# A gated attention stage: gates summed by a VectorE scan in place of triangle products, rows turned by DMA, and VectorE's work in another order

## The chip, the core and the metric

The kernel runs on one core of a Trainium2 chip. A core has five engines that run side by side, each with its own queue of instructions: TensorE (PE; its weight loads are listed as PEld), VectorE (DVE), ScalarE (ACT), GpSimd (POOL) and SyncE (SP), which here issues transfers. The metric is the device time of one execution in microseconds.

## The reference, cut to what matters

The model is two layers over x (16 batches of 256 tokens by 256 features). Layer 0 is a cross attention and an expert layer, layer 1 another cross attention and a gated linear attention. Only the last is touched by the change:

```python
gk1 = log_sigmoid(x @ Wg1a @ Wg1b + bg1) / 16      # first stream's gates, per token, head, feature
gk2 = log_sigmoid(x @ Wg2a @ Wg2b + bg2) / 16      # second stream's gates
fac, mfac = ...                                     # one of four experts per token, by softmax(x @ We)
o_dense  = gla(q1, k1, v, gk1)
o_sparse = sum over experts of gla(q2 * fac, k2 * fac, v, gk2 * mfac)
o = o_dense + o_sparse
o = o * rsqrt(mean(o * o) + eps) * norm_w * (g * sigmoid(g)),  g = x @ Wga @ Wgb
x = x + tanh(g_ffn[1]) * (o @ Wo)
```

`gla` is a linear attention with decays: with G the sum of the gates along the tokens up to t, the weight of token s for token t is (q exp(G_t)) . (k exp(-G_s)), for s at or before t. A constant added to all of G cancels, so the sum may start anywhere.

## The kernel before, in words

The stages run one after another, with the ends laid over each other; the last one is `stage3_fast` (from L1619). It treats one batch after another, and in each batch four pairs of heads; one pair is a step, `p` counts them from 0 to 63, `b = p // 4` is the batch and `m = p % 4` the step within it. All instructions of this stage are kept in the order in which the program issues them, on each engine, so the order written out in the loop `for p in range(last)` and in the tables `start`, `copies`, `middle`, `rest`, `late`, `behind_mask`, `by_rows` and `logs` (L2007 on) is the order of every engine's queue. A table entry such as `(route, 1)` under key 1 means: in step 1 of a batch, do `route` for the batch one ahead. Products are float32; the profile counts two instructions for each.

What a batch needs ahead of its steps is made during the steps of the batch before, or of the one before that:

- `stats` and `norm_ahead` give the normed rows `xn`, two batches ahead: VectorE's moments, four small POOL operations, then ScalarE's scaling. `turn_ahead` turns them to `xnT` (features by tokens) by sixteen VectorE transposes of 32 rows each.
- `lows` (step 0) multiplies `xnT` by the small first factors, and VectorE copies the result to `low`. A quarter of it is also wanted on other partitions: two VectorE operations make `low2`, and a transfer makes `lowd`.
- `all_gates` (step 1), `gates_end` and `gate_logs` (steps 1 and 2) make `lg` = log(1 + exp(-z)) for both streams, with tokens on the partitions. `steepest` keeps its largest entry for a check at the end of the kernel.
- `route_rows`, `route_logits` and `route_sums` (step 0) and `route` (step 1) choose the expert of each token, `turn_hot` and `turned_hot` (step 2) turn that choice, and `pairs` (step 2) makes the masks `em` (pairs of tokens of one expert, with the triangle) and `am`.
- `outgates` makes the output gate: four products, then ScalarE's exponents and copies `zs`, later a POOL product `gw`.

Within step p, TensorE goes through `keys_queries(p + 1)`, `decays(p + 1)`, the first stream's scores `products(p, 0)`, `values(p - 1)` (in steps 1 to 3, by `inside`), `second(p + 1)`, the second stream's scores `products(p, 1)`, and in step 0 only then `values` of the pair before. `decays` sums the gates by products: the gates `lg` are the weights and a triangle of -1/16 and 1/16 (`dmask`, 128 by 128 for each half of the tokens) is multiplied in for the first stream, `em` for the second; four ScalarE exponents read the two results from PSUM. VectorE multiplies the keys and queries by them (`factors`, `f`; `factors_second`, `q`), and POOL the second stream's keys (`k`). `masked(p, 0)` takes the first scores out of PSUM (VectorE, `at`), which frees the only bank pair `sc` for the second scores; `masked(p, 1)` takes those (four VectorE operations) in step p + 1, and POOL adds the two (`at<-at,at`) before `values(p)` can read them. `squares`, `gated`, `scaled` and `project` finish a batch in the steps of the next one.

Of the kernel before, what the change touches and what calls it, by code (L numbers as in the profile page):

```python
# [10 lines left out]
F32 = mybir.dt.float32  # L11
# [6 lines left out]
P = 128  # L18
# [36 lines left out]
def flamingo_kernel(tc: tile.TileContext, t, out):  # L55


    nc = tc.nc
    with tc.tile_pool(name="flag", bufs=1) as fp:
        check = {n: fp.tile(shape, F32, tag=n, name=n) for n, shape in (  # L60
            ("esum", [P, 2 * S]), ("rsum", [P, S]), ("most", [P, 2 * B]), ("uneven", [P, B]),
            ("gates", [P, 2 * B]), ("second", [P, 16]), ("logs", [P, 2 * B]),
            ("rows", [P, 2, 8]), ("rsum2", [P, 2 * B]), ("rsum0", [P, 4 * B]))}
        for x in check.values():
            nc.gpsimd.memset(x, 0.0)
        bad = check["bad"] = fp.tile([1, 1], I32, tag="bad", name="bad")
        layers(tc, t, out, check)
        with tc.If(nc.values_load(bad[0:1, 0:1], min_val=0, max_val=P,
                                  skip_runtime_bounds_check_because="a count of partitions") > 0):
            layers(tc, t, out, None)  # L70
# [3 lines left out]
def layers(ctx: ExitStack, tc: tile.TileContext, t, out, check):  # L74
# [1544 lines left out]
    def stage3_fast(early_bank):  # L1619

        with ExitStack() as sx:
# [25 lines left out]
            nc.sync.dma_start(out=lbg2[64:], in_=t["lbg"][:64, :])  # L1647
            low2 = w1.tile([64, P], F32, tag="low2", name="low2")
            wo = w1.tile([P, 4, D], F32, tag="wo", name="wo")

            hots = [w1.tile([P, 2, 4], F32, tag=f"hot{n}", name=f"hot{n}") for n in range(2)]

            xn, xnT, low, lg, hT, em, am, lowd = {}, {}, {}, {}, {}, {}, {}, {}
            v, gw, u_, oT = {}, {}, {}, {}
# [17 lines left out]
            def norm_ahead(b):  # L1672
                xn[b] = w0.tile([P, 2, D], F32, tag="xn", name="xn")
                normed(xn[b], xs[b], *mvs.pop(b))

# [8 lines left out]
            def turn_ahead(b):  # L1684

                xnT[b] = of(b).tile([P, 2, S], F32, tag="xnT", name="xnT")
                turned_squares(xnT[b], xn[b], range(16))

            def lows(b):

                low[b] = of(b).tile([P, 2, S], F32, tag="low", name="low")
                ps = bank("low")
                for c in range(2):
                    for k in range(2):
                        matmul(ps[:, c * S:(c + 1) * S], la[:, k, c * P:(c + 1) * P], xnT[b][:, k, :],
                                         start=k == 0, stop=k == 1)
                dve3.tensor_copy(low[b][:, 0, :], ps[:, :S])
                dve3.tensor_scalar(low[b][:, 1, :], ps[:, S:], vec[:, V_ONE:V_ONE + 1], None, ALU.add)
                lowd[b] = of(b).tile([P, S], F32, tag="lowd", name="lowd")
                nc.sync.dma_start(out=lowd[b][64:], in_=low[b][:64, 1, :])  # L1700
                if b > 0:
                    for r in range(0, 64, 32):
                        dve3.tensor_scalar(low2[r:r + 32, :], ps[64 + r:96 + r, S + P:],
                                           vec[64 + r:96 + r, V_ONE:V_ONE + 1], None, ALU.add)

# [38 lines left out]

            def gates(b, i):

                if i == 0:
                    lg[b] = of(b).tile([P, 2, 2, 512], F32, tag="lg", name="lg")
                for n, (lo, hi) in enumerate(((64, 81), (96, 113))):
                    ps = bank("z")  # L1750
                    matmul(ps, low[b][lo:hi, 1, tokens(i)], lbg[lo:hi, :], start=True, stop=True)
                    act3.activation(lg[b][:, i, n, :], ps, AF.Exp, scale=-1.0)

            def all_gates(b):

                lg[b] = of(b).tile([P, 2, 2, 512], F32, tag="lg", name="lg")
                two = psa.tile([P, 2, 512], F32, tag="sc", name="sc")
                one = [bank("z"), bank("z")]
                for i in range(2):
                    for n, (lo, hi) in enumerate(((0, 17), (32, 49))):  # L1760
                        x, w = (low2[lo:hi, :], lbg2[lo:hi, :]) if i else (low[b][64 + lo:64 + hi, 1, tokens(0)],
                                                                         lbg[64 + lo:64 + hi, :])
                        matmul(two[:, n, :] if i else one[n], x, w, start=True, stop=True)
                act3.activation(lg[b][:, 0, 0, :], one[0], AF.Exp, scale=-1.0)
                act3.activation(lg[b][:, 1], two, AF.Exp, scale=-1.0)
                z_[b, "z"] = one[1]

            def gates_end(b):
                act3.activation(lg[b][:, 0, 1, :], z_.pop((b, "z")), AF.Exp, scale=-1.0)

            def gate_logs(b, i):
                act3.activation(lg[b][:, i], lg[b][:, i], AF.Ln, bias=1.0)

            def steepest(b, i):
                dve3.tensor_reduce(check["gates"][:, 2 * b + i:2 * b + i + 1],
                                        lg[b][:, i].rearrange("p n f -> p (n f)"), AX.X, ALU.max)

# [29 lines left out]
            def outgates(b):  # L1807
# [7 lines left out]
                for h, ps in enumerate(two):  # L1815
                    e, zs = (w2.tile([P, 512], F32, tag=n, name=n) for n in ("eg", "zs"))
                    act3.activation(e, ps, AF.Exp, scale=-1.0)
                    act3.copy(zs, ps)
                    z_[b, h] = zs, e
# [22 lines left out]
            def decays(p):  # L1842

                b, m, cols = place(p)
                gq[p] = psu.tile([P, 512], F32, tag="gq", name="gq")
                gz[p] = psu.tile([P, 512], F32, tag="gz", name="gz")
                for n, (ps, mask) in enumerate(((gq[p], dmask), (gz[p], em[b]))):
                    for i in range(2):
                        matmul(ps[:, tokens(i)], lg[b][:, i, n, cols], mask[:, i, :], start=True, stop=True)
                    ee[p, n] = w2.tile([P, 2, S], F32, tag=f"ee{n}", name=f"ee{n}")  # L1850
                    act3.activation(ee[p, n][:, 0, :], ps[:, :S], AF.Exp)
                    act3.activation(ee[p, n][:, 1, :], ps[:, :S], AF.Exp, scale=-1.0)

# [23 lines left out]
            def shares_end(b):  # L1877
# [4 lines left out]
                flat = rd[b].rearrange("p x j -> p (x j)")  # L1882
                most = check["second"].rearrange("p (x j) -> p x j", j=2)
                dve3.tensor_tensor(most, most, den[:, :, 0::16], ALU.max)
                dve3.reciprocal(rd[b], den[:, :, 0::16])
# [64 lines left out]
            def squares(b, mp):  # L1950
                if mp == 0:
                    u_[b] = w2.tile([P, 4, S], F32, tag="u", name="u")
                    oT[b] = w2.tile([P, 4, S], F32, tag="oT", name="oT")
                ps = o.pop((b, mp))
# [50 lines left out]

            start = {2: [(turn_hot, 1)]}
            copies = {2: [(turned_hot, 1)]}  # L2007
            middle = {0: [(lows, 1)], 1: [(all_gates, 1)], 2: [(pairs, 1)], 3: [(scaled, 0, 0)]}

            rest = {0: [(bias, 2)], 1: [(route, 1)], 2: [(steepest, 1, 0), (stats, 2)], 3: [(steepest, 1, 1), (turn_ahead, 2)]}  # L2010
            late = {1: [(scaled, -1, 1)], 2: [(project, -1)], 3: [(vals, 1)]}
            behind_mask = {0: [(route_logits, 1)]}
            by_rows = {0: [(outgates, 0)], 1: [(gates_end, 1)]}
            logs = {0: [(route_sums, 1), (outgates_end, 0, 0)], 1: [(outgates_end, 0, 1), (gate_logs, 1, 0)], 2: [(gate_logs, 1, 1), (norm_ahead, 2)]}

# [15 lines left out]
            keys_queries(0)  # L2031
            for f, *a in ((turn_hot, 0), (turned_hot, 0), (stats, 1), (pairs, 0), (norm, 1), (steepest, 0, 0),
                          (steepest, 0, 1)):
                f(*a)
# [21 lines left out]
            for p in range(last):  # L2056
# [5 lines left out]
                if 0 < p:  # L2062
                    masked(p - 1, 1)
                run(copies, p)
                if p % 4 == 0:
                    shares_end(p // 4)
                if 1 < p and p % 2 == 1:
                    gated((p - 2) // 4, (p - 2) % 4 // 2)
# [13 lines left out]

                inside = p % 4 > 0 and p + 1 < last
                if inside:
# [17 lines left out]
            gated(b, 1)  # L2102
            ends.part("rsum", "gates", "rsum2", "rsum0")
            scaled(b, 1, dve3, [lambda: project_part(b, 1, 0), warm])
# [5 lines left out]
    class Verdict:  # L2110

        bounds = {"esum": E_MOST, "rsum": R_MOST, "most": E_MOST, "uneven": 0.5, "second": E_MOST, "logs": E_MOST,
                  "gates": G_MOST, "rows": ROWS + 0.5, "rsum2": R_MOST, "rsum0": R_MOST}

        def __init__(self):
            self.r, self.n = st.tile([P, 10], F32, tag="vr", name="vr"), 0

# [103 lines left out]
```

## Time and profile before

| | us |
|---|---|
| median of 3 runs (1840.51 to 1845.21) | 1845.09 |
| the profiled execution's own time | 1847.08 |
| its span, first to last instruction | 1845.3 |
| TensorE, VectorE busy in the span | 1813.5, 1231.5 |
| ScalarE, GpSimd busy in the span | 873.9, 1017.0 |
| a batch of the last stage, 1457.97 to 1495.68 | 37.71 |

The profile is of one execution. In a row of the groups, `x64` is the number of instructions, then come the busy time of all, the mean nanoseconds of one, and the idle time just before them with what ended it. An arrow names what is written and what is read. Nearly all lines are helpers (L50, L1637, L1640), so the names of the tiles tell which step of the program a row is. The chain is the work that ended last, followed back. In the timeline a row is start, length, engine, line, operation, and in square brackets the idle time before it. TensorE's instructions overlap: a product that lasts 0.38 us in its row may follow the one before by 0.11, so a run of products is measured by what it advances the chain.

### The profile page before, as it was taken

The page shows a single profiled execution, that of the slowest core. Times are in us where ns is not written, and L with a number is a line of the kernel's source. Part 1 is how long each engine was busy: PE and PEld are TensorE (multiplying, and loading weights), DVE is VectorE, ACT ScalarE, POOL GpSimd, SP SyncE. Part 2 cuts the span into 40 slices and gives each one's busy share as a digit, 9 for nine tenths or more (in the row PEclk, how much of TensorE's full clock was granted, in tenths as well). Part 3 has the DMA queues.
Part 4 walks back from the last instruction along what each step waited for, and adds up shares of the span by engine and source line. Part 5 has one row for each costly group of instructions (what it writes and reads, how often), then busy time and mean ns, then how long its engine had stood idle before and what let it go on. Part 6 is the DMA issues. An engine that isn't in the chain of part 4 may idle for free.

```text
span 1845.3 us, 35182 instructions
## 1 busy us (share of the span) xinstructions
PE 1813.5 (98%) x13870; PEld 1249.8 (68%) x13870; DVE 1231.5 (67%) x2903; ACT 873.9 (47%) x1804; POOL 1017.0 (55%) x1001
## 2 busy tenths in 40 slices
PE   8999999999999999999999999999999999999997
PEld 5666666666766667666777766656767777777765
DVE  3355656566665666656474488867888878878874
ACT  4433344433444334443433487846555645455543
POOL 4654767567676576756634767315444444444433
PEclk9999999999999999999999999999999999999999
DMA  9800010000010100000077933100000000000000
GB/s 304 226 1 22 16 34 15 25 17 23 23 37 8 29 19 10 31 23 18 13 248 238 233 49 49 18 4 3 14 8 10 8 10 13 8 9 8 14 9 14
DMA packets 68504, 85.86 MB, mean 47 GB/s; under 512 B 10740, under 2 KB 55908, under 8 KB 67818
## 3 DMA queue, kind: packets, MB, share of 16 engines
q1 hardware_dynamic: 56041, 66.74, 11.5%
q0 software_dynamic: 12288, 16.79, 4.5%
q8 instruction: 111, 1.82, 0.4%
q14 instruction: 64, 0.52, 0.1%
HBM read 44.17 MB, written 38.29 MB: 45 GB/s over the span
## 4 chain that ended last, share of the span: by engine, by line
PE 82%; POOL 9%; DVE 4%; issue 2%; ACT 2%; DMA 1%; SPq 0%; POOLq 0%; DVEq 0%; ACTq 0%
PE o L50 11%; PE qk L50 11%; PE v L50 8%; PE sc L50 8%; PE proj L50 7%; PE kq L1637 7%; PE sc L1637 5%; POOL es L50 4%; PE gq L1637 3%; PE v L1637 3%; PE o L1637 3%; PE proj L1637 3%; POOL x L50 2%; PE ex L50 2%; POOL rs L50 2%
## 5 line engine op out<-in xcount | busy, mean ns | idle before, releaser
L50 POOL TENSOR_SCALAR rs<-mv 128x2 f32<-128x2 f32 (+2 forms) x85 | 16.3, 192 | 376.8 <-DVE mv L50 371.1
L50 DVE RECIPROCAL rd<-o 128x256 f32<-128x256 f32 x64 | 112.3, 1755 | 164.0 <-PE o L50 123.7
L50 POOL TENSOR_TENSOR at<-at,at 128x768 f32<-128x768 f32 x63 | 114.1, 1812 | 142.4 <-DVE at L50 142.4
L50 ACT ACTIVATE e<-sc 128x1024 f32<-128x1024 f32 (+1 forms) x192 | 181.7, 1016 | 18.4 <-PE sc L50 18.4
L50 PE MATMUL sc<-qk 64*128 64x256 f32 (+1 forms) x1536 | 183.1, 384 | 0.5 <-DVE qk L50 0.5
L50 PE MATMUL o<-e,v 128*32 128x256 f32 (+1 forms) x3072 | 177.9, 379 | 0.0
L50 PEld LDWEIGHTS sc<-qk 64*128 64x128 f32 (+1 forms) x1536 | 132.0, 172 | 55.1 <-issue 26.8
L50 POOL TENSOR_TENSOR esum<-esum,es 128x512 f32<-128x512 f32 x128 | 163.5, 1277 | 10.0
L50 PE MATMUL qk<-kvT,wkv 128*128 128x333 f32 x512 | 164.3, 443 | 0.0
L50 ACT ACTIVATE qk<-qk 128x256 f32<-128x256 f32 x128 | 48.8, 381 | 231.4 <-PE qk L50 231.4
L50 POOL TENSOR_TENSOR es<-e 128x1024 f32<-128x1024 f32 x64 | 151.2, 2363 | 12.1 <-ACT e L50 9.0
L50 POOL TENSOR_TENSOR es<-es,e 77x1024 f32<-77x1024 f32 x64 | 150.4, 2350 | 5.0
L50 PEld LDWEIGHTS o<-e,v 128*32 128x32 f32 (+1 forms) x3072 | 99.9, 110 | 66.3
L50 PE MATMUL qk<-kvT,wq 128*128 128x256 f32 x512 | 134.6, 385 | 0.0
L50 DVE COPY qk<-qk 128x333 f32<-128x333 f32 x128 | 64.6, 504 | 93.8 <-ACT qk L50 92.8
L50 POOL DMA_INDIRECT x<-rows_out,pos x64 | 101.1, 1580 | 33.2 <-issue 17.0
L50 PEld LDWEIGHTS qk<-kvT,wq 128*128 128x128 f32 x512 | 94.3, 189 | 35.2 <-issue 9.6
L50 PEld LDWEIGHTS qk<-kvT,wkv 128*128 128x128 f32 x512 | 97.2, 190 | 30.0
L50 PE MATMUL proj<-wo0h,oT 128*128 128x256 f32 x512 | 113.7, 380 | 0.3 <-DVE oT L50 0.3
L50 PE MATMUL v<-wkv,kvT 128*128 128x512 f32 x256 | 113.1, 595 | 0.0
L50 PEld LDWEIGHTS proj<-wo0h,oT 128*128 128x128 f32 x512 | 95.9, 190 | 13.9 <-issue 0.8
L50 POOL DMA_INDIRECT rows<-xw,pos x64 | 66.8, 1043 | 61.1 <-ACT xT L50 24.0
(265 smaller groups left out, 4085.7 us busy)
## 6 DMA issues: line engine op xcount, KB each, us to landing
rows<-zero SPq DMA_DIRECT2D x16, 640.0 KB
xin<-rows SPq DMA_DIRECT2D x16, 640.0 KB
rows_out<-y SPq DMA_DIRECT2D x16, 384.0 KB
v<-vctx SPq DMA_DIRECT2D x15, 308.0 KB
x<-in_x_dram SPq DMA_DIRECT2D x16, 256.0 KB
rows_out<-y SPq DMA_DIRECT2D x16, 256.0 KB
out_dram<-x SPq DMA_DIRECT2D x15, 256.0 KB
wkv<-in_wkv_dram SPq DMA_DIRECT2D x2, 1024.0 KB
```

The lines of the kernel that those rows point to most:

```text
L50: x = getattr(self.engine, name)(*a, **k)
L1637: tc.keep_in_program_order(nc.tensor.matmul(*a, **k))
```

## The change

It has these parts, all in the last stage:

- **Gates.** The first stream's gates are made with features on the partitions (`lgT`, four tiles of 128 by 256) and summed along the tokens by a VectorE scan, one for each pair (`summed_gates(p + 2)`, behind `masked(p - 1, 1)`). POOL makes from the sum's middle entry two biases (`mid`), and ScalarE's two exponents read the sum with scale and bias. The triangle products go. A second check, `steps`, keeps the largest sums; `steepest` looks at the second stream only, once per batch.
- **Turned rows.** `norm_ahead` writes `xn` in another layout, one VectorE transpose turns all its 32 by 32 blocks, and sixteen transfers of SP's queue put the blocks in place. `low2` comes by one transfer.
- **Order.** `route` and `stats` move from the middle of steps 1 and 2 to the end of step 1, `norm_ahead` from the end to the middle of step 2, `turn_ahead` from step 3 to the end of step 2, `turn_hot` behind the keys and queries of step 2, `pairs` to the start of step 3. `values` of the last pair comes inside step 0 as well. The `zs` copies move from ScalarE to VectorE; a maximum in `shares_end` becomes a reduction; `oT` is `u` in place.

```diff
             def norm_ahead(b):
                 xn[b] = w0.tile([P, 2, D], F32, tag="xn", name="xn")
-                normed(xn[b], xs[b], *mvs.pop(b))
+                every = "p i (k d) -> p i k d"
+                normed(xn[b].rearrange("p k (i d) -> p i k d", i=2), xs[b].rearrange(every, k=2), *mvs.pop(b))
...
-                turned_squares(xnT[b], xn[b], range(16))
+                y = w1.tile([P, 4, P], F32, tag="turned", name="turned")
+                dve3.transpose(y.rearrange("p x d -> p (x d)"), xn[b].rearrange("p k d -> p (k d)"))
+                to = xnT[b].rearrange("p k (i s) -> p (k i) s", i=2)
+                for q in range(0, P, 32):
+                    for r in range(0, P, 32):
+                        nc.sync.dma_start(out=to[r:r + 32, :, q:q + 32], in_=y[q:q + 32, :, r:r + 32])
...
                 if b > 0:
-                    for r in range(0, 64, 32):
-                        dve3.tensor_scalar(low2[r:r + 32, :], ps[64 + r:96 + r, S + P:],
-                                           vec[64 + r:96 + r, V_ONE:V_ONE + 1], None, ALU.add)
+                    nc.sync.dma_start(out=low2, in_=low[b][64:, 1, :])
...
             def all_gates(b):
 
-                lg[b] = of(b).tile([P, 2, 2, 512], F32, tag="lg", name="lg")
+                lgT[b] = of(b).tile([P, 4, S], F32, tag="lgT", name="lgT")
+                lg[b] = of(b).tile([P, 2, 512], F32, tag="lg", name="lg")
                 two = psa.tile([P, 2, 512], F32, tag="sc", name="sc")
                 one = [bank("z"), bank("z")]
-                for i in range(2):
-                    for n, (lo, hi) in enumerate(((0, 17), (32, 49))):
-                        x, w = (low2[lo:hi, :], lbg2[lo:hi, :]) if i else (low[b][64 + lo:64 + hi, 1, tokens(0)],
-                                                                         lbg[64 + lo:64 + hi, :])
-                        matmul(two[:, n, :] if i else one[n], x, w, start=True, stop=True)
-                act3.activation(lg[b][:, 0, 0, :], one[0], AF.Exp, scale=-1.0)
-                act3.activation(lg[b][:, 1], two, AF.Exp, scale=-1.0)
+                matmul(one[0], low[b][96:113, 1, tokens(0)], lbg[96:113, :], start=True, stop=True)
+                matmul(one[1], low2[32:49, P:], lbg2[32:49, :], start=True, stop=True)
+                for m in (0, 2, 1, 3):
+                    x, w = (low2[0:17, :], lbg2[0:17, :]) if m >= 2 else (low[b][64:81, 1, :], lbg[64:81, :])
+                    matmul(two[:, m // 2, m % 2 * S:(m % 2 + 1) * S], w[:, m * P:(m + 1) * P], x, start=True, stop=True)
+                act3.activation(lg[b][:, 0, :], one[0], AF.Exp, scale=-1.0)
+                act3.activation(lgT[b], two.rearrange("p x (m s) -> p (x m) s", m=2), AF.Exp, scale=-1.0)
                 z_[b, "z"] = one[1]
...
+            def summed_gates(p):
+
+                b, m = p // 4, p % 4
+                x = lgT[b][:, m, :]
+                dve3.tensor_tensor_scan(x, ones[:, 0:1].to_broadcast([P, S]), x, 0.0, ALU.mult, ALU.add)
+                mid[p] = st.tile([P, 2], F32, tag="mid", name="mid")
+                pool3.tensor_tensor(mid[p], bc(x[:, P - 1], [P, 2], 1), sides, ALU.mult)
+                if m == 3:
+                    dve3.tensor_tensor(check["steps"], check["steps"], lgT[b][:, :, S - 1], ALU.max)
...
-                    act3.copy(zs, ps)
+                    dve3.tensor_copy(zs, ps)
...
-                gz[p] = psu.tile([P, 512], F32, tag="gz", name="gz")
-                for n, (ps, mask) in enumerate(((gq[p], dmask), (gz[p], em[b]))):
-                    for i in range(2):
-                        matmul(ps[:, tokens(i)], lg[b][:, i, n, cols], mask[:, i, :], start=True, stop=True)
+                ps = gz[p] = psu.tile([P, 512], F32, tag="gz", name="gz")
+                for i in range(2):
+                    matmul(ps[:, tokens(i)], lg[b][:, i, cols], em[b][:, i, :], start=True, stop=True)
+                c = mid.pop(p)
...
+                for x in range(2):
+                    act3.activation(ee[p, 0][:, x, :], lgT[b][:, m, :], AF.Exp, bias=c[:, x:x + 1],
+                                    scale=(1.0, -1.0)[x] / 16)
...
-                most = check["second"].rearrange("p (x j) -> p x j", j=2)
-                dve3.tensor_tensor(most, most, den[:, :, 0::16], ALU.max)
+                dve3.tensor_reduce(check["second"][:, b:b + 1], den[:, :, 0::16], AX.XY, ALU.max)
...
-            start = {2: [(turn_hot, 1)]}
-            copies = {2: [(turned_hot, 1)]}
-            middle = {0: [(lows, 1)], 1: [(all_gates, 1)], 2: [(pairs, 1)], 3: [(scaled, 0, 0)]}
-
-            rest = {0: [(bias, 2)], 1: [(route, 1)], 2: [(steepest, 1, 0), (stats, 2)], 3: [(steepest, 1, 1), (turn_ahead, 2)]}
+            start = {3: [(pairs, 1)]}
+            middle = {0: [(lows, 1)], 1: [(all_gates, 1)], 2: [(turn_hot, 1)], 3: [(scaled, 0, 0)]}
+
+            rest = {0: [(bias, 2)], 2: [(turned_hot, 1), (norm_ahead, 2)], 3: [(steepest, 1)]}
...
-            logs = {0: [(route_sums, 1), (outgates_end, 0, 0)], 1: [(outgates_end, 0, 1), (gate_logs, 1, 0)], 2: [(gate_logs, 1, 1), (norm_ahead, 2)]}
+            logs = {0: [(route_sums, 1), (outgates_end, 0, 0)],
+                    1: [(route, 1), (stats, 2), (outgates_end, 0, 1), (gate_logs, 1, 0)],
+                    2: [(gate_logs, 1, 1), (turn_ahead, 2)]}
...
                 if p % 4 == 0:
                     shares_end(p // 4)
+                if p + 2 < last:
+                    summed_gates(p + 2)
...
-                inside = p % 4 > 0 and p + 1 < last
+                inside = 0 < p and p + 1 < last
```

## The prediction

> **What bounds the kernel now.** I read the page's slices first, then the last stage cut at the starts of its four head-pair steps in one steady batch (1457.97 to 1495.68 us), then that batch's chain and each engine's timeline.
>
> ```profile
> PE 1813.5 (98%) x13870; PEld 1249.8 (68%) x13870; DVE 1231.5 (67%) x2903; ACT 873.9 (47%) x1804; POOL 1017.0 (55%) x1001
> ...
> PE   8999999999999999999999999999999999999997
> ...
> DVE  3355656566665666656474488867888878878874
> ```
>
> TensorE is full throughout; VectorE is fullest in the last third, which is the stage changed. The same batch by step 0 to 3, the columns being length, then busy time of PE, PEld, DVE, ACT and POOL:
>
> ```profile
> 1457.97:1467.35 9.38, 9.18 (x73) 7.35 (x71) 7.97 (x20) 3.02 (x9) 3.98 (x4) 1.00 0.03 7
> 1467.35:1475.25 7.90, 7.90 (x57) 5.15 (x56) 5.77 (x14) 7.08 (x17) 3.88 (x3) 1.00 0.01 2
> 1475.25:1485.55 10.30, 10.30 (x68) 8.18 (x66) 7.24 (x16) 4.25 (x10) 6.15 (x9) 1.00 0.07 25
> 1485.55:1495.68 10.13, 10.13 (x60) 6.43 (x59) 9.75 (x26) 5.87 (x13) 3.77 (x3) 1.00 0.01 2
> sum 37.71, PE 37.51 PEld 27.11 DVE 30.73 ACT 20.22 POOL 17.78; mean PE 9.38 PEld 6.78 DVE 7.68 ACT 5.05 POOL 4.45
> ```
>
> So a batch lasts 37.71 us and TensorE is its bound. Its product groups, with what they advance the chain: kq 1.92, low 1.73, triangle (gq) 0.45, second stream (gz) 0.45, z 1.05, ms 0.86, both 0.84, proj 3.46, v 3.44, first scores 0.85, o 0.80, second queries 0.64, second scores 0.65.
>
> ```profile
> 1462.22 0.45 PE gq L1637 x4
> 1462.67 0.45 PE gz L1637 x4
> ...
> 1463.13 0.27 PE sc L1640
> ...
> 1464.28 0.96 DVE at L50
> ```
>
> Two things to see: VectorE gets onto the chain only in step 0; and the tokens' turn (sc, L1640) starts at once behind gz because VectorE finished `low` just then.
>
> **TensorE's removals.** The four triangle matmul instructions advance the chain 0.45 us in each of 64 steps: 28.8 us at most. In `all_gates`, four 512-column instruction pairs become two and four 256-column ones: the same columns, 0. Moving `values` of the last pair inside step 0 puts 0.80 us of products where the chain now waits for `at`, emx and e: the restart (0.14 idle and 0.92 against 0.65) is worth 0.4 per batch.
>
> **VectorE's ledger per batch.** Out: sixteen transposes 5.04, two low2 pieces 0.70, one gates reduction 1.21, the held `second` 1.54 for a reduction of 0.16. In: one transpose 128x512, by the line through 128x64 at 0.240 and 128x256 at 0.440, 0.71; two zs copies at 0.69 (row of the 128x512 PSUM copy y), 1.38; one 128x4 maximum 0.17; four scans. No scan is in the trace. The nearest row, q, 128x256 in 0.415, bounds it below; the reciprocal of 128x256 (1.755) above. [...] From the rows q 0.415 and f (128x512) 0.681, a fixed 0.149 and twice 0.266 estimate 0.68; I take that, as the row q is no recurrence. Four: 2.72, against 1.66 by the row. VectorE then has 27.4 of some 37.7 us: not the bound, so only its moments matter.
>
> **Other queues.** ScalarE loses two zs copies (0.59 each) and reads two of four exponents from SBUF: nothing, being behind its own slack. POOL gains four 128x2 products, 0.2 each. The smaller memsets, the eleventh verdict and the shared oT buffer: under 0.5 in total, hidden but for one reduction at the end. SP gets sixteen issues for the turn and one for low2. `lowd` shows an issue of 0.47; sixteen need 7.5. On my walk below the transpose ends 28 us after the batch's start, so the last lands near 28 + 7.5 + 2 = 37.5, and its reader `low` starts 40.1 in: hidden with 2.6 to spare, while an issue stays under 0.63. [...] The trace's `lowd` spent about 4.1 engine-us on 80 packets, 51 ns each; 144 packets over 16 engines are 0.46 per transfer, so I take the row. low2 has 5 us until all_gates: hidden.
>
> **The moments, walked step by step.** What VectorE and POOL do to one another is in these lines:
>
> ```profile
> 1459.83 1.54 DVE L50 TENSOR_TENSOR second<-second,dens 128x16 f32<-128x16 f32 x1
> ...
> 1470.75 1.54 DVE L50 TENSOR_TENSOR eq<-e,em 128x8 f32<-128x8 f32 x1
> ```
>
> ```profile
> 1459.52 1.81 POOL L50 TENSOR_TENSOR at<-at,at 128x768 f32<-128x768 f32 x1 [5.31 <-DVE at L50]
> ...
> 1470.46 1.82 POOL L50 TENSOR_TENSOR at<-at,at 128x768 f32<-128x768 f32 x1
> ```
>
> Two-SBUF-operand VectorE operations of 0.17 us end just when POOL's add ends (1461.3, 1472.3). The scan also has two SBUF operands, so it can be held and can hold POOL's add in turn, which here always starts behind masked.
>
> *Step 0:* the scan waits for the add (to 3.4 after the batch's start), ends 4.1, before `low` is there at 4.26. The turn needs both `low` copies, which end where they do now; gz alone no longer fills the time. The 0.45 saved is idle. Order saves 0.4: 9.0.
>
> *Step 1:* zs copies delay masked by 1.3 us, to 2.1 behind step 1's start; all_gates wants its bank at 2.35. gw, then the scan, then the add end at 5.0; o is due at 5.4. First scores now meet the lg exponents (idle 0.1). 7.90 - 0.45 + 0.1 = 7.55.
>
> *Step 2:* `route` has moved behind q, which ends 7.45 after step 1's start. ScalarE's r ends at 6.95 as now, so POOL runs oT to 8.3 and k to 9.1, and route's first product and `eq` wait for these. Four more at 0.2: hot at 9.95. The turn of hot is due at 7.55 + 1.92 = 9.47: 0.5 idle. Behind route on VectorE stand stats (0.97) and masked (1.39), to 12.3; behind stats on POOL its four small operations (1.57), to 12.5, then gw (held by the 0.68 scan, 1.27) and the add (1.81), to 16.2. o is due at 10.0 + 0.31 + 0.64 + 3.46 + 0.85 = 15.25: 0.9 idle. ScalarE's norm_ahead ends about 13.6 and the factors after it 15, in time for f. The step: 10.30 - 0.45 - 0.84 (pairs moved out) + 1.4 = 10.4, and 0.3 more for gz behind a short product and restart: 10.7.
>
> *Step 3:* + 0.84 - 0.45: 10.5; the transposes' 5.04 gone, masked and at early, nothing late.
>
> Sum 9.0 + 7.55 + 10.7 + 10.5 = 37.75 against 37.71: about 0. Fourteen batches have this load, +0.6; the last two lack stats and route and keep about 1 and 1.8: total -2.2. The profiled execution took 1847.08, its span 1845.3, 1.8 around it; less 2.2 its own time is 1844.9. The runs' median, 1845.09, stands 2.0 below it, so **1843**.
>
> **Rivals.** *The waits don't form* (chance 0.24). Then a batch saves 0.38 + 0.35 + 1.29 - 0.39 = 1.63; 14 times, and 3 for the ends: 26, so 1819. For it: everything late in step 2 starts from 0.85 + 0.75 us in which route is held. Against: both `second` and `eq` are held in each batch now (mean 1541 and 1545).
>
> *The scan is slower* (0.22), the other side. Each 0.1 us beyond 0.68 delays `low` in step 0 (beyond 0.84) and the adds in steps 1 and 2, 0.2 to 0.3 per batch, 4 us in all. Slower by 0.3% begins near 0.9 us; at 1.2 it is 1863, at the reciprocal's 1.755 about 1886. [...]
>
> *The turned rows land late* (0.12). An issue of 0.78, as the fourfold cT burst shows (3.10), makes 12.5, landing 2.4 late in 14 batches: 1876. Against: most issues are 0.31 to 0.47.
>
> **How the numbers follow.** My forecast has 0.42 and its own range, 1834 to 1852, from the scan at 0.42 to 0.8 and either order of taking turns with POOL. A measurement can tell about 0.3%, 5.5 us. Of the 0.42, 0.12 fall below 1839.5, 0.24 within, 0.06 above. The first rival is all faster; of the scan's 0.22, 0.02 is within; the late rows are all slower: 0.36, 0.26, 0.38. Leaving out a tenth each side gives 1819 to 1868.
>
> **What would show it.** The triangle rows gone; step 1 shorter; in step 0 TensorE idle some 0.45 for `low`; in step 2 idle for hot and again for POOL's add; a scan of about 0.68 beside POOL; route's first product and eq at 0.8 instead of 0.17. Wrong would be: no idle in step 2, scans over 0.9, or `low` waiting for a DMA.

## The result, and the profile after

The changed kernel takes **1858.2 us** (median; 1856.66 to 1861.93) against 1844.07 (1840.51 to 1845.21) for the kernel before, measured beside it: a ratio of 1.0085, 95% interval 1.0073 to 1.0097. It is slower by 14 us, where the forecast was 1843. The profiled execution, the slowest of the four, took 1861.93; its span is 1860.1, 14.8 more than the span before.

First the page of the changed kernel: busy time of the engines, then the slices.

```profile
PE 1801.7 (97%) x13678; PEld 1236.0 (66%) x13678; DVE 1224.4 (66%) x2761; ACT 872.6 (47%) x1772; POOL 1048.9 (56%) x1068
...
PE   8999999999999999999999999999999999999997
...
DVE  3355656566666666655573488867777877777775
...
PEclk9999999999999999999999999988999999999999
```

TensorE works 11.8 us less, but the span is 14.8 longer. Besides, the granted clock has two slices at 8, where the last stage begins; before, it had none:

```profile
PEclk9999999999999999999999999999999999999999
```

Next, a steady batch of the last stage, cut at its four steps, in the columns of the table of before (length, then busy time of PE, PEld, DVE, ACT and POOL, clock, DMA):

```profile
1470.66:1479.78 9.12, 8.65 (x67) 6.78 (x67) 7.33 (x16) 2.83 (x9) 4.47 (x5) 1.00 0.10 20
1479.78:1487.67 7.89, 7.89 (x55) 5.32 (x55) 7.50 (x15) 6.36 (x15) 4.14 (x4) 1.00 0.00 1
1487.67:1498.14 10.47, 9.28 (x61) 7.27 (x59) 7.92 (x22) 5.81 (x13) 7.07 (x10) 1.00 0.08 27
1498.14:1508.57 10.43, 10.43 (x59) 6.62 (x62) 6.94 (x13) 5.12 (x12) 4.19 (x4) 1.00 0.15 21
```

The four lengths add up to 37.91 us; forecast were 37.75, before were 37.71. TensorE is idle 0.47 in step 0 and 1.19 in step 2. For whom it waits, the waits of TensorE over the batches from 1290 to 1800 us say (us in total, times, longest):

```profile
PE o L1637 <- POOL at L50: 10.7, 13, 0.8
PE sc L1640 <- DVE low L50: 6.0, 13, 0.5
PE hT L1640 <- ACT lgT L50: 4.8, 13, 0.4
PE hT L1640 <- DVE hot L50: 1.4, 1, 1.4
PE low L1637 <- DMA xnT<-turned: 1.0, 2, 0.6
```

The same view of before has one line:

```profile
PE sc L1637 <- DVE e L50: 2.4, 13, 0.2
```

The third wait of the changed kernel carries ScalarE's name; `hot`, which the transposes read, ended at 1489.89 and lgT's logarithm at 1489.91 in the batch above, so this view can't tell them apart.

**Where the 14.8 us are.** Cut at the starts of den in each batch: up to the first, 1236.91 against 1235.20, +1.7. The first batch, 42.80 against 34.14, **+8.7**. The other fourteen, 533.78 against 528.02, +5.8: a batch takes 37.93 at least (14 times 0.21 is 3.0), and seven of them take 0.1 to 0.8 more (2.8). The end: -1.3. So over half lies in one batch out of sixteen, behind this wait in its step 2:

```profile
1262.93 1.55 PE L1637 MATMUL o<-at,v 128*64 128x256 f32 x8 [2.96 <-POOL at L50]
```

It looks like this in slices of 5 us, 1255 to 1280:

```profile
1255.00:1260.00 5.00, 4.20 (x32) 3.28 (x28) 4.68 (x19) 2.56 (x5) 1.95 (x5) 1.00 0.02 5
1260.00:1265.00 5.00, 2.07 (x10) 1.28 (x12) 1.65 (x2) 2.81 (x7) 3.71 (x4) 0.66 0.00 0
1265.00:1270.00 5.00, 5.00 (x20) 3.83 (x17) 2.52 (x6) 1.45 (x3) 0.00 (x0) 0.50 0.07 12
1270.00:1275.00 5.00, 5.00 (x17) 3.17 (x16) 3.02 (x6) 1.97 (x5) 2.76 (x3) 0.81 0.19 26
1275.00:1280.00 5.00, 5.00 (x41) 2.89 (x39) 2.06 (x4) 2.63 (x8) 1.47 (x2) 1.00 0.13 18
```

TensorE's busy time falls to 2.07 of 5 us, because o waits 2.96 for POOL's add; then the clock stands at half for some 10 us (1261.63 to 1271.87). Another stretch at 0.50 to 0.88 lies at 1235 to 1245, behind idle times of 0.60, 0.88 and 0.47, and one of 3.41 us begins at 1220.67. Between 1190 and 1290 us the kernel before shows only one of that length, 0.82 and 0.84 at 1210 to 1220. Elsewhere the two are alike: both have low clock at 1055 to 1065 and in their last 25 us.

Every run has its mean granted clock, so what the clock takes can be estimated as time times (1 - clock): 13.5 us for the changed kernel (0.9928, mean of its runs), 5.8 for the kernel before (0.9969, 27 runs beside later experiments). By this estimate about 8 of the 14 us are clock, and the rest waits. The two profiled executions, at 0.991 and 0.995, give 7.5. The changed kernel's four runs go from 1861.93 at 0.991 to 1856.66 at 0.995, so the profiled one shows more of the clock than the others have. The estimate is rough: an experiment below brings it down by 6.7 and the time by 3.

### The profile page after: what moved, and what is told of

The parts are those of the page before. It is cut to its first block, busy times and chain, and to the rows that moved or that the text cites. A ratio compares the mean times of both kernels' runs of the same rounds, so it can differ in the third digit from the quotient of the medians.

```text
span 1860.1 us, 34963 instructions
## 1 busy us (share of the span) xinstructions
PE 1801.7 (97%) x13678; PEld 1236.0 (66%) x13678; DVE 1224.4 (66%) x2761; ACT 872.6 (47%) x1772; POOL 1048.9 (56%) x1068
## 4 chain that ended last, share of the span: by engine, by line
PE 73%; POOL 13%; DVE 8%; issue 3%; SPq 1%; ACT 1%; DMA 1%; POOLq 0%; DVEq 0%; ACTq 0%
PE o L50 11%; PE qk L50 11%; PE sc L50 8%; PE v L50 8%; PE proj L50 7%; PE kq L1637 5%; PE sc L1637 4%; POOL es L50 4%; POOL rs L50 3%; PE v L1637 3%; POOL x L50 2%; PE o L1637 2%; PE gq L1637 2%; PE low L1637 2%; PE ex L50 1%
## 5 line engine op out<-in xcount | busy, mean ns | idle before, releaser
L50 POOL TENSOR_SCALAR rs<-mv 128x2 f32<-128x2 f32 (+2 forms) x85 | 16.2, 190 | 347.8 <-DVE mv L50 346.0
L50 POOL TENSOR_TENSOR at<-at,at 128x768 f32<-128x768 f32 x63 | 125.2, 1987 | 151.6 <-DVE at L50 151.6
L50 ACT ACTIVATE e<-sc 128x1024 f32<-128x1024 f32 (+1 forms) x192 | 181.5, 1015 | 18.5 <-PE sc L50 18.5
L50 DVE TENSOR_TENSOR at<-sc,amask 128x768 f32<-128x768 f32 x64 | 61.2, 957 | 75.2 <-PE sc L1637 75.2
```

What stands on the lines that cost most here:

```text
L50: x = getattr(self.engine, name)(*a, **k)
```

## The experiments

Each ratio is to the kernel before, run on the same chip, with its 95% interval. "Batch" is the steady distance between two starts of den in the trace.

### POOL's gate product first

```diff
-                    1: [(route, 1), (stats, 2), (outgates_end, 0, 1), (gate_logs, 1, 0)],
+                    1: [(route, 1), (outgates_end, 0, 1), (stats, 2), (gate_logs, 1, 0)],
```

> The changed kernel with one order altered: in step 1 the end of the second output gate (POOL's gw) goes ahead of the row statistics of the second-next batch, so that POOL no longer runs four small products on those statistics before gw and the add at. Nothing is left out. My theory (the wait of the head products o in step 2, 0.82 us in every batch and 2.96 us in the first, is POOL's order): about 13 times 0.8 less, 10 us, and in the first batch 1.3 us of wait and part of the slow-clock products, 2 to 4 us: 1844 to 1848 against 1858. Rival (the statistics are then late in their turn, the normed rows come 1 to 2 us later and so do the turned rows, which already land late in some batches): the 0.8 reappears as a wait of low for a transfer, and the time stays within 4 us of 1858.

Measured: 1856.91 us, 1.0065 [1.0052, 1.0079]; batch 38.09. TensorE's waits, 1290 to 1800:

```profile
PE hT L1640 <- DVE hot L50: 19.8, 14, 1.4
PE sc L1640 <- DVE low L50: 6.0, 13, 0.5
```

The wait for POOL's add is gone from these batches, and one of 1.4 us for hot has come in, named so by the profile. The likely cause is one that the changed kernel shows in its last batch but one, where gw comes as early: beside gw (1793.86, 1.27) a product of route (eq, 1793.94) takes 1.21 instead of 0.17. Neither reason was the right one. The time hardly moves, as the rival said, but not for late rows: step 2 has one chain over VectorE **and** POOL (q, route, statistics, gw, add), and its order on POOL only chooses which reader waits.

### Products in the first batch's wait

```diff
                 inside = 0 < p and p + 1 < last
+                if p == 2:
+                    ps = bank("warm")
+                    for _ in range(7):
+                        matmul(ps, ones, v[0][:, 0, :], start=True, stop=True)
```

> The changed kernel with seven 128x512 products more, whose result nothing reads, in the first batch's step 2, where TensorE waits 2.96 us for POOL's at and where the granted clock then falls to 0.50 to 0.66. Nothing is left out. Theory (the wait lowers the clock, and the products behind it at half rate cost some 4.3 us): the clock stays near 1.00 in that batch and the time falls 3 to 5 us, to 1853 to 1855. Rival (the clock falls there for another reason, a budget over the whole chip or a fixed period): no change or, with the additional products, 0 to 2 us more, 1858 to 1860.

Measured: 1858.6 us, 1.0076 [1.0062, 1.009]. The clock was at 1.00 there, but the seven products took 6.2 us, more than the wait of 2.96. With three of them:

> The changed kernel with three 128x512 products whose result nothing reads in the first batch's step 2. (Seven of them took 6.2 us, 0.44 for each of two passes, 3.2 us more than the wait; the clock stayed at 1.00 there, but the surplus ate the gain.) Three take 2.66 us and end inside the 2.96 us wait. Nothing is left out. Theory (the low clock is due to this wait and costs some 4 us): the clock stays at 1.00 between 1255 and 1280 us, the first batch is 3 to 4 us shorter than in the changed kernel, and the whole 1853 to 1856. Rival (the low clock moves to another place): within 1 us of 1858.

Measured: 1855.14 us, 1.006 [1.0047, 1.0072]; the first batch 38.66 instead of 42.80. Its slices behind the filled wait:

```profile
1260.00:1265.00 5.00, 5.00 (x30) 3.92 (x29) 3.84 (x10) 1.95 (x4) 0.54 (x1) 1.00 0.07 12
1265.00:1270.00 5.00, 5.00 (x24) 2.57 (x24) 1.90 (x3) 3.79 (x9) 3.66 (x4) 1.00 0.19 26
```

The wait itself ends where it did; the products behind it run at full clock, and the run is 3 us shorter. So the low clock there is due to the idle time. The clock's mean rises from 0.9928 to 0.9963, which the estimate above would make 6.7 us.

### The rows turned by VectorE again

```diff
-                y = w1.tile([P, 4, P], F32, tag="turned", name="turned")
-                dve3.transpose(y.rearrange("p x d -> p (x d)"), xn[b].rearrange("p k d -> p (k d)"))
...
-                        nc.sync.dma_start(out=to[r:r + 32, :, q:q + 32], in_=y[q:q + 32, :, r:r + 32])
+                turned_squares(xnT[b], xn[b], range(16))
```

> The changed kernel with one part undone: the normed rows of the second-next batch are turned by sixteen 32-row transposes of VectorE at the same place, and no transfer carries them. Nothing is left out. Theory (the sixteen transfers, at 0.64 us from one issue to the next, are late for low in some batches, 2.7 us over the run): those batches return to 37.93 us, and the time falls 2 to 3 us, to about 1856. Rival (the 4.3 us more of VectorE work in steps 2 and 3 make masked and at late): 0.5 to 1.5 us per batch more, 1865 to 1880.

Measured: 1882.0 us, 1.0206 [1.0192, 1.022]; batch 40.0. TensorE's waits, 1290 to 1800:

```profile
PE gz L1637 <- DVE em L50: 23.5, 13, 1.9
PE o L1637 <- POOL at L50: 10.7, 13, 0.8
```

The rival came true, 2 us over its range and at another reader. No batch is late by a transfer any more, but em, which gz reads in step 3, stands behind the transposes: since pairs moved to step 3, the place of the old transposes is no longer free. The transfers are worth 24 us in this order.

### The triangle products again

`gates`, `all_gates`, `decays` and `steepest` as before the change, `summed_gates` out:

```diff
-                if p + 2 < last:
-                    summed_gates(p + 2)
...
-                    matmul(ps[:, tokens(i)], lg[b][:, i, cols], em[b][:, i, :], start=True, stop=True)
+                for n, (ps, mask) in enumerate(((gq[p], dmask), (gz[p], em[b]))):
+                    for i in range(2):
+                        matmul(ps[:, tokens(i)], lg[b][:, i, n, cols], mask[:, i, :], start=True, stop=True)
```

> The changed kernel with one part undone: the first stream's gates are summed along the tokens by the four triangle products per step again, and there is no scan, no 128x2 product of POOL and no maximum over the scans' ends. The order of the work, the turned rows by transfer and zs on VectorE are kept. Nothing is left out. Theory (the scans are nearly worth the products they replace: 0.45 x 4 = 1.8 us per batch come back, less 0.47 of low's wait and 0.3 to 0.8 of the waits in step 2): 0.5 to 1.0 us per batch more than the changed kernel, 1866 to 1874. Rival (the scans, which POOL holds up to 1.86 us and which hold POOL, are what makes the changed kernel slow): less than the changed kernel, 1840 to 1855.

Measured: 1851.56 us, 1.0042 [1.003, 1.0054]; batch 37.84. The rival came true. With 64 times 0.45 us of products **more**, the kernel is 6.6 us faster. Its waits of TensorE from 1290 to 1800 us are a single one:

```profile
PE hT L1640 <- DVE hot L50: 0.8, 1, 0.8
```

So in this order of work all three waits per batch come with the scans, and take back the whole 1.8 us. And the clock is 0.9958 here, which by the estimate above is 5.8 of the 6.6 us. It fits that products which seem worth removing also fill places where TensorE would idle. But the wait in the first batch is hardly shorter:

```profile
1252.87 0.87 PE L1637 MATMUL o<-at,v 128*64 128x256 f32 x8 [2.45 <-POOL at L50]
```

So most of this wait comes with the order, not with the scan (nor with the turned rows: without them it is 2.96 as well). The timelines point to `stats`: POOL's four operations on the statistics, from 1257.80 on in the changed kernel, run ahead of gw (1259.84) and the add (1261.07); in the kernel before they begin at 1257.58, behind the add (1253.97), and o doesn't wait there. No run moves `stats` back alone. The clock stayed at 1.00 here, and the first batch takes 36.45, still 2.3 over the kernel before.

### Route back in step 1, and the maximum with one operand

```diff
-            rest = {0: [(bias, 2)], 2: [(turned_hot, 1), (norm_ahead, 2)], 3: [(steepest, 1)]}
+            rest = {0: [(bias, 2)], 1: [(route, 1)], 2: [(turned_hot, 1), (norm_ahead, 2)], 3: [(steepest, 1)]}
...
-                    1: [(route, 1), (stats, 2), (outgates_end, 0, 1), (gate_logs, 1, 0)],
+                    1: [(stats, 2), (outgates_end, 0, 1), (gate_logs, 1, 0)],
```

> The changed kernel with one move undone: route (the choice of the next batch's experts) is back in step 1 ahead of the masked scores, instead of behind f and q. Nothing is left out. Theory (in step 2 VectorE's small operations of route, 0.84 to 1.4 us of them held by POOL, make hot 0.37 late and the statistics behind them, and so POOL's at, 0.82 late): hot's wait goes whole, at's by 0.3 to 0.8, 0.7 to 1.2 per batch, and 1847 to 1850 against 1858. Rival (route in step 1 is held by POOL's add and pushes the masked scores by 1.2 us, and their add at): a wait of the head products in step 1 takes the place, 1856 to 1866.

Measured: 1846.8 us, 1.002 [1.0013, 1.0027]; batch 37.34.

```profile
PE sc L1637 <- DVE at L50: 7.0, 13, 0.5
PE sc L1640 <- DVE low L50: 6.0, 13, 0.5
```

Both waits of step 2 are gone, one of 0.54 has come into step 1. The theory came true, with a part of the rival. In front of that new wait, on VectorE, stand these in the changed kernel as well (with POOL's add, which holds them):

```profile
1482.02 1.19 DVE L50 TENSOR_TENSOR_SCAN lgT<-ones,lgT 128x256 f32<-128x256 f32 x1
1483.24 1.59 DVE L50 TENSOR_TENSOR steps<-steps,lgT 128x4 f32<-128x4 f32 x1
```

```profile
1482.62 2.19 POOL L50 TENSOR_TENSOR at<-at,at 128x768 f32<-128x768 f32 x1
```

The maximum over four numbers per row ends when the add ends (1484.83 and 1484.81). It looks the same as `second` and `eq` in the kernel before, 1.54 each beside the add. So the next edit, on top of the last:

```diff
-                    dve3.tensor_tensor(check["steps"], check["steps"], lgT[b][:, :, S - 1], ALU.max)
+                    dve3.tensor_reduce(check["steps"][:, b:b + 1], lgT[b][:, :, S - 1], AX.X, ALU.max)
```

> The same as the run before it, and besides the maximum over the scans' ends is a reduction with one operand into a column per batch (it was an operation with two SBUF operands, 1.59 us because POOL holds it, in step 1). Nothing is left out. Theory (route then fits into the time in which VectorE was held or idle in step 1, and everything in step 2 comes 2 to 3 us earlier): both waits of step 2 go, 1.2 per batch over 14 batches and more than 1 in the first batch: 1838 to 1843, at or under the kernel before. Rival (route itself waits for POOL's add instead, as its first product and eq did in the kernel before, and nothing is won by the reduction): within 2 us of the run before it.

Measured: **1833.6 us**, 0.994 [0.9928, 0.9952]; batch 36.67. The reduction takes 0.16. Better than forecast, and faster than the kernel before. Two small edits are worth 24.6 us.

### The rows turned earlier

```diff
-            rest = {0: [(bias, 2)], 1: [(route, 1)], 2: [(turned_hot, 1), (norm_ahead, 2)], 3: [(steepest, 1)]}
+            rest = {0: [(bias, 2)], 1: [(route, 1)], 2: [(turned_hot, 1), (norm_ahead, 2), (turn_ahead, 2)], 3: [(steepest, 1)]}
...
-                    2: [(gate_logs, 1, 1), (turn_ahead, 2)]}
+                    2: [(gate_logs, 1, 1)]}
```

> The run with route back in step 1 and the one-operand maximum (1833.6 us), and besides the transpose of the next rows, and so their sixteen transfers, 4 us earlier, in step 2 behind hT's copy, where VectorE is idle until the projection. Nothing is left out. Theory (low waits for the transfers in about half of the batches, 3 to 4 us over the run, because the sixteen issues start too late): every batch from the second on takes 36.67, and the whole 1829.5 to 1831. Rival (the lateness is a matter of the issue rate or of other transfers in the way, not of the start): within 1 us of 1833.6.

Measured: 1832.67 us, 0.9943 [0.9929, 0.9956]. In the trace the theory holds: every batch from the second on takes 36.66 to 36.68, where the run it builds on had six longer ones, 3.0 us together. By the time alone the rival fits as well, since only 0.9 of the 3 us is seen there. The issues of SyncE in one batch (start, and what all sixteen took), of that run and then of this one:

```profile
1484.57 10.76 SPq L1696 DMA_DIRECT2D xnT<-turned  x16
```

```profile
1475.40 10.64 SPq L1696 DMA_DIRECT2D xnT<-turned  x16
```

The rate is the same; the start is not: the issue of lowd, behind the products low that need these rows, comes 15.2 us after it there (1499.74) and 19.6 here (1494.95). The intervals of the two times overlap, and the clock was 0.9944 here and 0.9955 there, by the same estimate 2 us the other way.

### The turn of low behind the scores

```diff
-                if n == 0 and m == 0 and b + 1 < B:
-                    route_rows(b + 1, ps[:, 1, 384:])
                 for lo, hi, i in ((0, S, 0), (P, S, 1)):
...
+                if n == 0 and m == 0 and b + 1 < B:
+                    route_rows(b + 1, ps[:, 1, 384:])
                 z_[p, n, "sc"] = ps
```

> The run with route back in step 1 and the one-operand maximum (1833.6 us), and besides the two transposes of low are issued behind the first scores of step 0 instead of ahead of them. Nothing is left out. Theory (TensorE idles 0.47 in each batch for low since the triangle products no longer lie in front; the first scores, 0.85, need nothing of low): 0.45 less per batch, 36.2 each, 15 times, 6 to 7 us: 1826 to 1828. Rival (the scores' reader on VectorE or their factors set the step's end, and the idle time only moves): within 2 us of 1833.6.

Measured: 1827.6 us, 0.9917 [0.9903, 0.993]; batch 36.13. The theory came true: 0.54 less per batch, 6 us in the time. The wait was worth its whole length, since scores that need nothing of low could stand in front.

### All that helped, and the same with triangle products

The four edits and the three products of the first batch together:

> The changed kernel with all that helped: route back in step 1, the one-operand maximum, the rows turned earlier, low's transposes behind the first scores, and three products whose result nothing reads in the first batch's step 2. Nothing is left out. Theory (the gains are of separate waits and add up): 14 batches at 36.2 us and a first batch of 37 to 38: 1820 to 1824, 1.1% to 1.3% under the kernel before. Rival (they share one slack, or a new wait takes the place): 1826 to 1834.

Measured: **1824.78 us**, 0.9904 [0.9889, 0.9919]; batch 36.13, the first batch 36.32. TensorE's waits from 1290 to 1800:

```profile
PE sc L1637 <- DVE at L50: 0.4, 1, 0.4
PE o L1637 <- POOL at L50: 0.2, 1, 0.2
```

They add up, short of the range by 0.8. With triangle products and no scan in the same order:

> The same as the run before it, but with the first stream's gates summed along the tokens by triangle products and no scan (so no maximum over scan ends either). Nothing is left out. Theory (without waits the scan is worth what the products cost on TensorE, 0.45 x 4 per batch, 28.8 us in all less what the ends keep): 37.8 to 38.0 us per batch, 1844 to 1850, which is 24 to 28 us more than the run before it. Rival (the scan's hold-ups on VectorE and POOL cost most of that in any order): less than 12 us more.

Measured: 1843.9 us, 1.001 [1.0002, 1.0019]; batch 37.75. **This is what the scan is worth: 1.62 of the 1.8 us per batch**, once hardly anything waits, and 19 us in the time. The gate products of step 1 take 1.54 in both, so they have no part in the difference. The traces' batches say 23.9 (14 times 1.62 and 1.23 in the first); the clock gives 4 back, 0.9976 with triangle products against 0.9952 without. By the means of the runs, 1845.0 and 1824.8, it is 20.2 and 4.3 of clock. And the order with turned rows alone, without the scan, is worth nothing against the kernel before.

### The copies zs on ScalarE

In the changed kernel, step 1 has no idle time of TensorE, but its gate products run differently. The timeline of TensorE in that step, before and after:

```profile
1469.24 0.70 PE L1637 MATMUL z<-lbg,low 17*128 17x512 f32 x2
1469.25 0.70 PE L1637 MATMUL sc<-lbg,low 17*128 17x512 f32 x2
1469.77 0.59 PE L1637 MATMUL z<-lbg,low 17*128 17x512 f32 x2
1469.78 0.59 PE L1637 MATMUL sc<-lbg,low 17*128 17x512 f32 x2
1470.31 0.71 PE L1637 MATMUL gq<-dmask,lg 128*128 128x128 f32 x4
```

```profile
1481.63 0.70 PE L1637 MATMUL z<-lbg,low 17*128 17x512 f32 x2
1482.16 0.48 PE L1637 MATMUL sc<-low,lbg 17*128 17x256 f32 x2
1482.17 0.59 PE L1637 MATMUL z<-lbg,low 17*128 17x512 f32 x2
1482.48 0.81 PE L1637 MATMUL sc<-low,lbg 17*128 17x256 f32 x6
1483.22 0.71 PE L1637 MATMUL gz<-em,lg 128*128 128x128 f32 x4
```

Before, a product of 17 rows into z and one into sc start within 0.01 us of each other and run side by side: 1.07 for all four. After, the first z runs alone, because the bank sc is read by masked until 1482.11, behind the two copies zs: 1.59. The 0.52 us are a wait, but TensorE counts as busy.

```diff
-                    dve3.tensor_copy(zs, ps)
+                    act3.copy(zs, ps)
```

> The changed kernel with one part undone: the two copies zs of the second output gate's sums are ScalarE's again (0.59 each) instead of VectorE's (0.69 each). Nothing is left out. Theory (VectorE in step 1 is 1.3 us freer, but the scan, the maximum and route behind it still wait for POOL's add, and POOL's gw waits for ScalarE's exponents, which come 1.2 us later): within 3 us of the changed kernel, 1855 to 1861. Rival (the copies on VectorE are what makes the chain of step 2 late): 1.0 per batch less, 1842 to 1848.

Measured: 1857.27 us, 1.0068 [1.0055, 1.0082]; batch 37.89. The theory came true on the time. The products are back in pairs, 1.07:

```profile
1477.30 0.70 PE L1637 MATMUL z<-lbg,low 17*128 17x512 f32 x2
1477.31 0.70 PE L1637 MATMUL sc<-low,lbg 17*128 17x256 f32 x4
```

But within the same step most of it is lost again: from the first gate product to o TensorE takes 3.83 (1477.30 to 1481.13), where the changed kernel takes 3.95.

To see whether the gain is only swallowed by step 2's waits, the same edit in the kernel with all that helped:

> The kernel with all that helped (1824.8 us, 36.13 per batch), and besides the two copies zs back on ScalarE. In it, as in the changed kernel, the gate products of step 1 take 1.54 to 1.59 us instead of the 1.07 of the kernel before, because two of them wait for the bank that VectorE's masked scores free 0.5 us late, behind zs; with zs on ScalarE they took 1.07 in the changed kernel, but the waits of step 2 swallowed the gain. Nothing is left out. Theory (with those waits gone the 0.5 counts): 35.6 to 35.7 per batch, 7 us less over the run: 1816 to 1820. Rival (ScalarE, with 1.2 us more ahead of the exponents of step 2, becomes late and takes it back): 1823 to 1828.

Measured: 1826.53 us, 0.9907 [0.989, 0.9923]; batch 36.32, 0.19 more than without.

```profile
PE sc L1637 <- DVE at L50: 2.5, 13, 0.2
```

The time is the rival's: the products take 1.06, but behind them gz, ms and the scores stand further apart (gz to ms 0.74 instead of 0.54, and 0.57 instead of 0.26 ahead of the second scores), and a small wait for VectorE has come back. One candidate is ScalarE's exponent of the bank sc: with and without the edit it ends 2.67 behind the first gate product, and the first scores, which write sc again, start at 2.86 with it and 3.04 without, so TensorE meets that exponent when it comes 0.5 earlier. That is read from the two timelines and no run tests it. Whoever has the copies, the times lie within 2 us of each other.

## Why the prediction was wrong

The wide range, 1819 to 1868, held the time and slower had the largest chance, but the forecast was 15 us off and outside its own range, 1834 to 1852. That the wide range held is luck: its upper part was there for a slower scan, which didn't come, and for rows landing late, which gave 2.6 us. By the forecast's own steps:

- **"Fourteen batches have this load, +0.6": this is the step that failed.** With the last two batches it makes 2.2 less in the span; 14.8 more came, and 8.7 of that in one batch. The sum is made of steady batches, and the first batch isn't one. There project and the ms of an earlier batch are missing, under which POOL's chain (rs, gw, at) lies in the others; the wait for the add is 2.96 us instead of 0.82, and the clock drops on it. The working gave this batch 0.04 us like any other. Of its 8.7, 4.1 are gone when the wait is filled, and 2.3 stand with triangle products too, so they are the order's.
- **"The last two lack stats and route and keep about 1 and 1.8"**: the last but one took 0.4 more, and the end is 1.3 shorter. Without `stats` in front of it, POOL's gw (1793.86, 1.27) runs beside route's products, one of which (eq, 1793.94) takes 1.21 instead of 0.17, and hot comes late, as in the run with the gate product first:

```profile
1795.89 0.38 PE L1640 MATMUL hT<-ident,hot 128*4 128x128 f32 x2 [1.42 <-DVE hot L50]
```

- **The clock stood in no term of the sum.** The triangle products were booked as cost alone. By the estimate from the mean clocks, the scan goes with more lost clock than triangle products in the same order: 13.5 us against 7.7, and with nearly all waits closed 8.7 against 4.4. Only for the first batch do the runs show which idle time does it. At the head the clock drops in one of the two kernels with triangle products as well (0.79 and 0.53 at 1225 to 1235 us).
- **"Sixteen need 7.5"**, at 0.47 an issue: the issue takes 0.60 and the next one starts about 0.65 after it, 10.3 for sixteen (10.32 at 1460.83), over the 0.63 that I had given as the limit. The rival "turned rows land late" was right in kind: late in six of fourteen batches, 2.6 us in the profiled execution, not 33; the seventh longer batch is the one late for hot. The row `lowd` was of a transfer with fewer packets: 80 by my count, while the changed kernel's 32495 packets more under 512 B are at most 145 for each of its 224 transfers of turned rows. SyncE's issue, 0.60 of each 0.65, sets the pace here.
- **"In `all_gates` ... the same columns, 0"**: 0.52 per batch. Equal columns, but not in pairs, as the bank comes late. Step 1 took 7.89 instead of 7.55.
- **"One 128x4 maximum 0.17"**: 1.59, held by POOL like `second`, although I had shown `second` and counted its removal as a gain. In the changed order it cost little, since VectorE then waits for scores anyway; it is what kept route from fitting into step 1.
- *Right:* the batch, 37.75 against 37.91 to 37.93, though step 1's excess is in part made up by step 2, and by the waits foretold: low 0.45 (0.47), hot 0.5 (0.37), POOL's add 0.9 (0.82). The add's end, 16.2 us behind step 1's start, is 16.16 in the trace. Steps 0, 2 and 3 are within 0.25. The scan at 0.68: no run had shown the factor two in that estimate, which was an assumption; the 64 scans of the changed kernel show a median of 0.684, which is 0.149 and 2.01 times 0.266, so **the rival "the scan is slower" is out**. Its mean is 1.1, because it takes longer beside POOL: 1.19 in step 1, where gw (1481.39, 1.26) is still running, and 1.85 in step 0, beside the add (1472.24, 1.81).
- *The rival "the waits don't form"* is out for the changed kernel. When the order is mended, low's wait included, which this rival had kept, a batch lies 1.58 under the kernel before (its 1.63), and the time 18.5 us under it (its 26).

## What to carry to other kernels

Where a stage repeats, walk its first round on its own: what hides a chain there may belong to a round that doesn't exist yet, and idle time of TensorE can be paid a second time through its clock (here a wait of 2.96 us was followed by 10.2 us at 0.50, and with the wait filled the first batch was 4.1 us shorter). Work taken off the bounding engine is worth only what the readers behind it can follow, so look for the small two-operand VectorE operations that stand beside a long POOL operation: here one of them rewritten (1.59 us, then 0.16), and route moved, made a loss of 14 us into a gain of 10. And a TensorE without idle time can still wait, when products that ran in pairs run one by one (1.59 us instead of 1.07).

## What the runs showed of the hardware

- **In the first batch the clock fell behind some waits and stayed up behind longer ones.** Behind the wait for POOL's add it fell to 0.50 for 10.2 us after 2.96 us (changed kernel) and after 2.29 (route back, one-operand maximum), for 6.8 us after 2.30 (turn of low behind the scores), for 3.4 us after 2.60 (route back), and not at all after 2.45 (triangle products) and 2.32 (rows turned earlier). In the trace of the changed kernel the stretches at half rate begin at 1056.83, 1220.67, 1234.33, 1261.63 and 1855.55 us, which are 48, 4, 8 and 174 times 3.413 us apart; the four that the kernel's end doesn't cut last 6.83, 3.41, 6.83 and 10.24. In that of the kernel before they begin 46, 179 and 5 times 3.413 us apart, and the three that end last 6.83, 3.41 and 3.41. In the 3.41 us ahead of the first four starts in the changed kernel TensorE was busy for 1.31, 3.41, 2.06 and 0.98, so a share below which the clock falls can't be given from these runs. One and the same kernel (route back, one-operand maximum) ran once at 0.993, 1838.91 us, and five times at 0.996, 1831.18 to 1834.17.
- **Some VectorE operations with two SBUF operands took longer beside POOL operations in these traces, and POOL's add took longer beside a scan.** A maximum over 4 numbers per row took 1.59 beside POOL's add, a product of 8 numbers per row 1.21 beside gw (0.17 in the other batches), and a scan 1.85 beside the add (0.68 in steps 2 and 3). The add took 2.13 and 2.19 where a scan had begun 0.16 and 0.60 before it, and 1.80 to 1.82 in the other two steps.
- In the changed kernel a transfer of 16 KB from SBUF to SBUF, of 32 rows with four pieces of 128 bytes each, took SyncE 0.60 us to issue (median of 224), and sixteen took 10.3 to 11.3 us, 0.65 to 0.71 each; single ones took up to 1.57.
- ScalarE's exponent of 128x256 took 0.495 with its input and bias from SBUF, and 0.372 from PSUM without a bias (means of 126 each in the changed kernel).
